# Two residual convolutions on one core: layer 2's row combinations on ScalarE and on adding transfers, reflections on GpSimd, and one buffer for statistics pieces

## The chip, the cores and the metric

The kernel runs on one core of a Trainium2 chip. A core has five engines that each work through their own list of instructions in order: TensorE (PE in the profile), VectorE (DVE), ScalarE (ACT), GpSimd (POOL) and SyncE (SP). SyncE computes nothing here: it issues the loads and stores. GpSimd issues transfers as well. The metric is the device time of one execution, in microseconds (us); lower is better.

## The reference

The input `x` is 8 images of 32 channels with 252 x 252 pixels in float32, and there is a 32 x 32 x 5 x 5 weight for each of two layers. Each layer is a group normalization, a 5x5 convolution with reflected borders and a residual addition. Cut to what is computed (the reference does the convolution through an FFT, which gives the same numbers):

```python
def gn(v):                                   # 16 groups of 2 channels, eps 1e-5, no affine part
    g = v.reshape(B, 16, 2, 252, 252)
    m, s = mean(g, over=(2, 3, 4)), var(g, over=(2, 3, 4))
    return ((g - m) / sqrt(s + 1e-5)).reshape(v.shape)

x = x + conv5x5(pad_reflect(gn(x), 2), L0_conv_weight)      # layer 1 (l = 0 in the code)
x = x + conv5x5(pad_reflect(gn(x), 2), L1_conv_weight)      # layer 2 (l = 1 in the code)
```

The mean and the variance are those of a whole image, so the convolution of an image's layer 1 can't be scaled before every pixel of the image was read once (the *statistics pass*), and layer 2 of an image can't start before layer 1 of that image is done.

## The kernel before, in words

**Layout.** An image is split by the parity of row and column into four phases. Phase and channel together make 4 x 32 = 128 partitions, and a 5x5 convolution over pixels becomes a 3x3 convolution over 126 x 126 blocks with 128 inputs and 128 outputs. The columns direction is done by three shifted matmuls (`product`, line 685). The rows direction uses a fast algorithm with six points, which makes four output block rows from six input block rows: points 1 to 4 give the sums and differences from which all four rows are made, and points 0 and 5 add what the two *outer* rows (the first and fourth of each group of four) need beside.

**Tiles and slots.** A *chunk* is 16 block rows (`ROWS`, four groups of four, `NT = 4`). An image has 8 chunks, so there are 8 images x 2 layers x 8 chunks = 128 tiles. Each has a *slot* in a list called `order`: first image 0's layer 1 alone, then chunk by chunk layer 1 of image b+1 alternating with layer 2 of image b, at last image 7's layer 2. A pair of slots in the alternating part is thus a layer 1 tile followed by a layer 2 tile or the other way about. Most tiles do points 0 and 5 with a second fast algorithm along the columns (`by_columns`): VectorE makes sums and differences of neighbouring columns (`columns`, line 619 and on), TensorE multiplies them (line 707) into the banks `sums` and `extra`, and VectorE puts the parts together (`column_parts`, lines 806 to 809).

**The input transform of a layer 2 tile** starts from `y`, the layer 1 result of 16 block rows, which stays in SBUF. It needs two sorts of row combinations:

- the *row sums* `v`, each row plus the row two further on. GpSimd's queue does these with transfers: one copies `y` to `v` (line 557), two add the shifted rows to it in place (lines 559 and 560, `accum_op=ALU.add`). `v` has one buffer, named `va`, so the copy of one layer 2 tile waits until VectorE has read the `v` of the tile before for the last time (line 609).
- the *row combinations* `u1` and `u2`: in each group of four rows, four times the second row plus the fourth, and four times the third row plus the first row of the next group. VectorE does these (`row_quads`, lines 576 and 577; `last_rows`, line 584, for the group that ends at the chunk's end).

From these VectorE makes the six points: `point2` (line 592), `point4` (596), `point3` (599), `point1` (602) and `points05` (609). For a layer 1 tile the same functions read the loaded rows `xs`, and VectorE makes `v` itself (line 567).

**The output of a tile.** ScalarE copies the finished banks of points 2 and 4 into the banks of points 1 and 3 (the *seeds*, lines 729 and 731), on top of which TensorE then adds points 1 and 3; copies points 2 and 4 out to `sd` (line 737); and VectorE makes differences and inner rows from them. In layer 1, ScalarE writes the outer rows into `y` (lines 787, 799) and squares them for layer 2's statistics (884). In layer 2, `outer_out` (line 778) has ScalarE copy the outer rows from PSUM right into the tile that is stored, four copies a tile; the inner rows go through `y` and are put into place by ScalarE in two pairs of copies, `interleave("inner", 0)` and `interleave("inner", 1)` (line 958). SyncE stores both (`send`, line 966). Every layer 1 tile also gets reflected border columns: `reflect` (lines 893 to 896), four copies by ScalarE, each of one column, 16 elements per partition; an image later its layer 2 tile reads them.

**Statistics of the next image.** While an image's layer 1 runs, the next image is read in 14 pieces of 128 x 1134 (`load_piece`, its transfer on line 254, issued by SyncE), and ScalarE passes over each twice (`piece_sums`): a sum (line 235) and a sum of squares (line 241). Chunks 0 to 6 have two pieces each, piece 2c in the layer 1 slot and piece 2c+1 in the slot after it. The pieces have two buffers (pool `spool`, tag `st`), and a piece is loaded two places ahead: right after pass p, piece p+2 is loaded.

**What sets the order.** Nothing is scheduled by a planner. `at(t, fn)` puts a function into a table under a nominal time; at the end the table is sorted by these times and each engine gets its instructions in that order (`tc.manual_schedule`). The nominal times set the order alone: what an instruction waits for while the program runs is decided by the data and by the buffers. `begin(i)` is the nominal begin of slot i; `t0` and `t1` are times within the slot. On SyncE one list holds, in order, the loads of input rows (`xs` and the last two rows `xtail`, line 143, for a chunk two layer 1 tiles on, which wait for the tile's earlier readers such as lines 577 and 584), the statistics pieces (254) and the stores (966). GpSimd's list holds the borders of loaded rows (lines 148 to 154), the addition of the residual to the weights (483), and the issue of the `v` transfers.

Of the kernel before, what the change touches and what calls it, by code (L numbers as in the profile page):

```python
# [42 lines left out]
F32 = mybir.dt.float32  # L43
BF16 = mybir.dt.bfloat16
AF = mybir.ActivationFunctionType
# [4 lines left out]
P = 128  # L50
# [6 lines left out]
def tile_conv_preact_x2(ctx: ExitStack, tc: tile.TileContext, x: bass.AP, w0: bass.AP, w1: bass.AP, out: bass.AP):  # L57
# [15 lines left out]

    const = ctx.enter_context(tc.tile_pool(name="const", bufs=1))
    xpool = ctx.enter_context(tc.tile_pool(name="xpool", bufs=2))
    spool = ctx.enter_context(tc.tile_pool(name="spool", bufs=2))
    ypool = ctx.enter_context(tc.tile_pool(name="ypool", bufs=9))
    tpool = ctx.enter_context(tc.tile_pool(name="tpool", bufs=2))
    vpool = ctx.enter_context(tc.tile_pool(name="vpool", bufs=1))
# [12 lines left out]
    def at(t: float, fn, *args, **kw):  # L92
        table.append((t, len(table), fn, args, kw))
# [151 lines left out]
    def load_piece(b: int, i: int):  # L245
        src = x[b].rearrange("ch h w -> (ch h w)").rearrange("(p n) -> p n", p=P)
        if b == 0:
            t = ypool.tile([P, PIECE], F32, tag="y", name=f"st_{b}_{i}")
        else:
            t = spool.tile([P, PIECE], F32, tag="st", name=f"st_{b}_{i}")  # L250
        parts = 3 if (b, i) == (0, NPIECE - 1) else 1
        m = PIECE // parts
        for j in range(parts):
            S.dma_start(t[:, j * m : (j + 1) * m], src[:, i * PIECE + j * m : i * PIECE + (j + 1) * m])
        pieces[b, i] = t
# [281 lines left out]
    def transform(t0: float, t1: float, b: int, l: int, c: int, free: float = -100.0, now=(0, 0, 0)):  # L537

        wi = WIN[l]
        got = {}  # L540
        sent = l == 1 and (b, c) != (0, 0)

        def source():
            if l == 0:
# [4 lines left out]
        def row_sums(add: bool):  # L549

            t, nxt = source()
            if not add:

                i = max(order.index((b, l, c)) - order.index((B - 2, 1, NCH - 2)), 0)
                got["v"] = vpool.tile([P, ROWS, wi], F32, tag=("va", "v")[i % 2], name=f"v_{b}_{l}_{c}")
                got["vt"] = got["v"].rearrange("p (t i) w -> p t i w", i=4)
                G.dma_start(got["v"], t)  # L557
            else:
                G.dma_start(got["v"][:, 0 : ROWS - 2], t[:, 2:ROWS], accum_op=ALU.add)  # L559
                G.dma_start(got["v"][:, ROWS - 2 : ROWS], nxt[:, 0:2], accum_op=ALU.add)  # L560

        def row_pairs(j0: int = 0, j1: int = NT):
            if j0 == 0:
# [67 lines left out]
        if (b, l, c) == order[0]:  # L631
            at(t0 - 33.3, row_quads, 0, 2)
            at(t0 - 31, point2, 0, 2)
            for fn in (row_pairs, point4):
                at(t0, fn, 0, 2)
            at(t0 + 0.2, row_quads, 2, 4)
            at(t0 + 0.2, row_pairs, 2, 4)
            at(t0 + 0.2, last_rows)
            at(t0 + 0.2, point2, 2, 4)
            at(t0 + 0.2, point4, 2, 4)  # L640
            at(t0 + 4.9, point1)
            at(t0 + 5.5, point3)
            at(t0 + 6.2, points05)
        else:
            if sent:
                two = begin(order.index((b, l, c)) - 2)
                at(two + 1.45, row_sums, False)
                at(two + 8.4, row_sums, True)
            else:
                at(t0, row_pairs)  # L650
            for dt, fn in ((2, row_quads), (3.2, last_rows), (3.6, point2)):
                at(t0 + dt, fn)
            at(max(t0 + 4.2, free + 9.45) if sent else t0 + 4.2, point4)
            at(max(t0 + 5.5, free + 7.8), point1)
            at(max(t0 + 5.6, free + (11.1 if by_columns(*now) else 10.25)), point3)
            at(t1, points05)
            if by_columns(b, l, c):
                at(t1 + 1.5, columns)
# [208 lines left out]
    def keep(t1: float, t2, b: int, c: int, got):  # L867
# [17 lines left out]

        def reflect():
            lo, hi = (1 if c == 0 else 0), (ROWS - 1 if c == NCH - 1 else ROWS)
            y, copy, r = got["y"], A.copy, slice(lo, hi)

            def negated(dst, src):  # L890
                A.activation(dst, src, AF.Copy, scale=-1.0)

            copy(y[:, r, 0:1], y[:, r, 1:2])
            copy(y[0:64, r, NB + 1 : NB + 2], y[0:64, r, NB : NB + 1])
            copy(y[64:128, r, NB + 1 : NB + 2], y[64:128, r, NB - 1 : NB])
            copy(y[:, r, NB + 2 : NB + 3], y[:, r, 2:3])
            if c == 0:
                negated(y[:, 0, :], y[:, 1, :])
                t = ytail[b] = small.tile([P, 2, WMAX], F32, tag="ytail", name=f"ytail_{b}")
                negated(t, y[:, 2:4, :])  # L900
            if c == NCH - 1:
                for cp in range(2):
                    negated(y[quad(cp, 0), ROWS - 1, :], y[quad(cp, 0), ROWS - 2, :])
                    negated(y[quad(cp, 1), ROWS - 1, :], y[quad(cp, 1), ROWS - 3, :])
# [33 lines left out]
    def last_but_one(b: int, c: int) -> bool:  # L938

        return (b, c) == (B - 1, NCH - 2)  # L940

    def out_tile(b: int, c: int, name: str):

        pool, tag = (spool, "st") if last_but_one(b, c) else (opool, "o")
        return pool.tile([P, NT, 2 * WOUT[1] + 2], F32, tag=tag, name=f"o_{name}_{b}_{c}")

    def store(t1: float, t0: float, b: int, c: int, got, from_y: bool):
# [23 lines left out]
        if from_y:  # L971
            for k, t in enumerate((0, 3.3)):
                at(t0 + t, interleave, "outer", k)
        for k, t in enumerate((t1 + 7.0, t1 + 7.2) if end else (t0 + 5.8, t0 + 7.8) if from_y else (t0 + 3.3, t0 + 5.8)):
            at(t, interleave, "inner", k)
        at(t0 + (4.6 if from_y else 2.6), send, "outer")
        at(t1 + 7.3 if end else t0 + 9.1, send, "inner")
# [41 lines left out]
    def begin(i: int) -> float:  # L1019

        return sum(10.2 + (own + [0.0])[j] + (late[j - 1] if j else 0.0) for j in range(i))
# [56 lines left out]
    for i, (b, l, c) in enumerate(order):  # L1078
# [36 lines left out]
        if l == 0 and b + 1 < B:  # L1115
            wide = 1 if b == 0 else 2
            if c == 0:
                for j in range(2):
                    at(begin(i - 1) + 1.0 if b > 1 else t0 + (8.0 if b else 1.0), load_piece, b + 1, j)
            if c < NPIECE // 2:  # L1120
                for j in range(2):
                    p = 2 * c + j
                    t = (t1 if wide == 2 and j else t0) + (8.6 + 2.5 * j if wide == 1 else 9.8)
                    if b == 1 and p < 4:
                        t = begin(NCH + (1, 1, 2, 2)[p]) + (9.8, 12.4, 9.8, 15.5)[p]
                    at(t, piece_sums, b + 1, p)
                    if p + 2 < NPIECE:
                        at(t + 2.6, load_piece, b + 1, p + 2)
            if c == 2:
                at(t0 + 14, fetch_weights, b + 1, 0)  # L1130
            if c == NCH - 1:
                finish_stats(b + 1, 0, *(t0 + t for t in (1.55, 4.4, 4.5, 6.9 if b else 7.7, 7.8, 8.4)))
                for j, ks in enumerate(pairs):
                    at(t0 + (9.5, 10.4, 11.3)[j], scale_points, b + 1, 0, ks)
                    at(t0 + (10.4, 12.3, 14)[j], lambda b=b, ks=ks: add_residual(G, scaled[b + 1, 0], ks))
# [43 lines left out]
```

## Time and profile before

| | us |
|---|---|
| three runs | 1912.64, 1910.19, 1912.46 |
| their median | 1912.46 |
| the profiled execution, its own time | 1912.64 |
| its span from first to last instruction | 1910.9 |
| TensorE, busy | 1850.6 (97% of the span) |
| VectorE, busy | 1736.1 (91%) |
| ScalarE, busy | 1491.1 (78%) |
| GpSimd, busy | 400.6 (21%) |

The mean clock granted to TensorE was 0.993 of full speed. Data moved at a mean of 193 GB/s: SyncE's queue took 49.6% of the time of the 16 DMA engines, GpSimd's queue 28.8%.

How to read the lines that follow: each names an engine, a line of the kernel's source, an operation, what it writes and reads (`out<-in`), and shapes as partitions x elements. In a list by time, the first column is the start and the second the duration, both in us, and a bracket at the end tells how long the engine had been idle before and for what it waited (`<-DVE sums L809`: for line 809 on VectorE). `x4` says that four instructions of that kind followed one another. SPq and POOLq are the issuing of transfers by SyncE and GpSimd.

### The profile page before, as it was taken

The page shows a single profiled execution, that of the slowest core. Times are in us where ns is not written, and L with a number is a line of the kernel's source. Part 1 is how long each engine was busy: PE and PEld are TensorE (multiplying, and loading weights), DVE is VectorE, ACT ScalarE, POOL GpSimd, SP SyncE. Part 2 cuts the span into 40 slices and gives each one's busy share as a digit, 9 for nine tenths or more (in the row PEclk, how much of TensorE's full clock was granted, in tenths as well). Part 3 has the DMA queues.
Part 4 walks back from the last instruction along what each step waited for, and adds up shares of the span by engine and source line. Part 5 has one row for each costly group of instructions (what it writes and reads, how often), then busy time and mean ns, then how long its engine had stood idle before and what let it go on. Part 6 is the DMA issues. An engine that isn't in the chain of part 4 may idle for free.

```text
span 1910.9 us, 20250 instructions
## 1 busy us (share of the span) xinstructions
PE 1850.6 (97%) x5194; PEld 961.6 (50%) x5194; DVE 1736.1 (91%) x3028; ACT 1491.1 (78%) x2661; POOL 400.6 (21%) x855
## 2 busy tenths in 40 slices
PE   5999999999999999999999999999999999999998
PEld 4444454545554555544555445554455545545455
DVE  7988799999999999989999999999999999998786
ACT  5886788878887888788897788877888866765576
POOL 4543011141112211122111311113111131110211
PEclk7999999999999999999999999999999999999999
DMA  9877588878788877987878967888878876676786
GB/s 273 205 174 183 137 212 205 193 205 217 186 207 205 195 201 180 222 211 177 214 182 202 227 178 204 190 204 204 197 207 182 210 180 142 155 180 155 179 210 136
DMA packets 207109, 369.06 MB, mean 193 GB/s; under 512 B 19088, under 2 KB 173968, under 8 KB 196752
## 3 DMA queue, kind: packets, MB, share of 16 engines
q1 hardware_dynamic: 178832, 230.73, 49.6%
q0 software_dynamic: 27600, 134.20, 28.8%
q10 hardware_dynamic: 560, 2.83, 0.4%
q8 instruction: 41, 0.67, 0.2%
q14 instruction: 76, 0.62, 0.1%
HBM read 167.15 MB, written 67.39 MB: 123 GB/s over the span
## 4 chain that ended last, share of the span: by engine, by line
PE 63%; DVE 13%; ACT 12%; issue 5%; DMA 2%; ACTq 0%; SPq 0%; DVEq 0%; POOL 0%
PE pairs L685 24%; PE m L685 19%; PE sums L685 6%; ACT o_outer L778 6%; PE sums L707 5%; PE extra L707 5%; PE extra L685 4%; DVE sd L748 1%; DMA out_dram<-o_inner 1%; ACT pairs L729 1%; ACT st L235 1%; DVE d L622 1%; DVE t L602 1%; DMA out_dram<-o_outer 1%; ACT junk L884 1%
## 5 line engine op out<-in xcount | busy, mean ns | idle before, releaser
L685 PE MATMUL pairs<-t,u 128*128 128x504 f32 (+2 forms) x1548 | 696.6, 588 | 23.6 <-ACT pairs L729 18.1
L685 PE MATMUL m<-t,u 128*128 128x508 f32 (+3 forms) x1560 | 676.2, 582 | 2.0 <-DVE u L526 2.0
L685 PEld LDWEIGHTS pairs<-t,u 128*128 128x128 f32 x1548 | 287.2, 189 | 351.8 <-issue 294.7
L685 PEld LDWEIGHTS m<-t,u 128*128 128x128 f32 x1560 | 294.7, 190 | 316.6 <-issue 294.3
L778 ACT COPY o_outer<-sums 64x512 f32<-64x512 f32 (+1 forms) x242 | 218.6, 903 | 102.9 <-PE sums L685 78.8
L707 PE MATMUL extra<-sdiff,wc 128*128 128x252 f32 (+3 forms) x680 | 173.1, 376 | 7.9 <-DVE sdiff L619 6.6
L707 PEld LDWEIGHTS extra<-sdiff,wc 128*128 128x128 f32 x680 | 125.4, 189 | 104.2 <-issue 59.7
L737 ACT COPY sd<-m 128x504 f32<-128x504 f32 (+2 forms) x258 | 136.2, 578 | 53.0 <-DVE sums L809 42.6
L748 DVE SCALAR_TENSOR_TENSOR sd<-sd,pairs 128x504 f32<-128x504 f32 (+2 forms) x258 | 163.6, 672 | 13.4 <-PE pairs L685 8.6
L958 ACT COPY o_inner<-y 64x508 f32<-64x508 f32 x248 | 165.4, 667 | 6.4 <-DMA out_dram<-o_inner 2.6
L884 ACT ACTIVATE junk<-y,negk 128x1008 bf16<-128x1008 f32 (+1 forms) x144 | 147.3, 1023 | 25.9 <-PE extra L707 15.9
L557 POOL DMA_DIRECT2D v<-y x63 | 35.7, 567 | 610.7 <-DVE t L609 555.1
L609 DVE SCALAR_TENSOR_TENSOR t<-v 128x1024 f32<-128x1024 f32 (+1 forms) x128 | 158.3, 1237 | 5.7 <-PE sums L685 5.7
L707 PE MATMUL sums<-d,u 128*128 128x252 f32 (+3 forms) x680 | 157.3, 373 | 0.0
L707 PEld LDWEIGHTS sums<-d,u 128*128 128x128 f32 x680 | 127.4, 189 | 25.1 <-issue 8.1
L685 PE MATMUL sums<-t,u 128*128 128x508 f32 (+5 forms) x312 | 133.2, 575 | 0.0
L567 DVE TENSOR_TENSOR v<-xs 128x1792 f32<-128x1792 f32 (+1 forms) x65 | 129.8, 1997 | 1.2
L148 POOL COPY xs<-xs 64x4 f32<-64x4 f32 (+3 forms) x113 | 51.3, 454 | 378.8 <-DMA xs<-in_x_dram 282.2
L241 ACT ACTIVATE st<-st,negk 128x1134 f32<-128x1134 f32 x98 | 121.7, 1242 | 3.2
L729 ACT ACTIVATE pairs<-m,means 128x504 f32<-128x504 f32 (+1 forms) x129 | 84.2, 653 | 50.4 <-PE m L685 46.5
L559 POOL DMA_DIRECT2D v<-y x63 | 54.3, 862 | 330.0 <-DMA v<-y 330.0
L159 ACT COPY xs<-xs 64x1792 f32<-64x1792 f32 (+2 forms) x97 | 109.6, 1132 | 13.5 <-POOL xs L151 11.3
(180 smaller groups left out, 2626.0 us busy)
## 6 DMA issues: line engine op xcount, KB each, us to landing
v<-y POOLq DMA_DIRECT2D x63, 1032.0 KB, 5.8
st<-in_x_dram SPq DMA_DIRECT2D x111, 567.0 KB, 6.8
v<-y POOLq DMA_DIRECT2D x63, 903.0 KB, 7.5
xs<-in_x_dram SPq DMA_DIRECT2D x96, 441.0 KB, 7.4
out_dram<-o_inner SPq DMA_DIRECT2D x241, 126.0 KB, 6.8
out_dram<-o_outer SPq DMA_DIRECT2D x226, 126.0 KB, 3.9
xs<-in_x_dram SPq DMA_DIRECT2D x44, 504.0 KB, 13.0
u<-ud SPq DMA_DIRECT2D x15, 1152.0 KB, 6.1
```

The lines of the kernel that those rows point to most:

```text
L159: copy(t[64:128, :, 0:256:2], t[0:64, :, 1:256:2])
L241: A.activation(junk, src, AF.Square, bias=negk, accum_out=acc[:, 1, i : i + 1])
L567: (V.tensor_add if l else V.tensor_sub)(v[:, r0:r1], t[:, r0 + 2 : r1 + 2], t[:, r0:r1])
L609: stt(t, got["vt"][:, :, 0:2], 4.0 if l else -4.0, got["vt"][:, :, 2:4], ALU.mult, ALU.add)
L685: T.matmul(dst, u[:, k, 2 - i, :], rhs[:, j0 + i0 : j0 + i1, i : i + wo], start=(i == 0 and not add), stop=(i == 2), skip_group_check=add,)
L707: T.matmul(dst[:, 0, use], w, rhs[:, use], start=(i == 2), stop=True, skip_group_check=(i != 2))
L729: A.activation(dst, src, AF.Identity, bias=norm[b, l][1][:, 0:1])
L737: A.copy(got["sd"][:, 1 + e], m24[e][:, 0:n])
L748: stt(d, d, -2.0, pairs13[e][:, 0:n], ALU.mult, ALU.add)
L778: (eng.copy if eng is A else eng.tensor_copy)(dst, src)
L884: A.activation(dst, src, AF.Square, bias=negk, scale=1.0 if i else -1.0, accum_out=acc[:, 1, at_ : at_ + 1])
L958: copy(got[name][halves[k], 0:n, cp : 2 * WOUT[1] : 2], got["y"][halves[cp], i : 4 * n : 4, :])
```

## The change

- `spool` has one buffer instead of two. For the pieces of images 2 to 7, piece p+1 is loaded right after pass p instead of piece p+2, and one piece instead of two is loaded ahead of the first pass (from image 3 on, 3 us later in nominal time). Image 1's pieces are still loaded two places ahead; they alternate between `spool` and the buffer `va`, which layer 2 does not need yet.
- For a layer 2 tile whose predecessor in `order` is a layer 1 tile (`sent_u`; 53 tiles: chunks 2 to 7 of image 0, all chunks of images 1 to 5, and chunks 0 to 6 of image 6) VectorE's `row_quads` and `last_rows` fall away. In their place ScalarE writes four times the second and third row of each group into a new tile `ua` (`four_times`), two slots ahead, and GpSimd issues three transfers that add the other rows to it (`outer_rows`), right behind the additions to `v`.
- The four `reflect` copies of chunks 1 to 6 are done by GpSimd instead of ScalarE.
- The pair of inner copies `interleave("inner", 1)` of a layer 2 tile whose outer rows come from PSUM takes the nominal time 3.3 us into the slot that `interleave("inner", 0)` had; `interleave("inner", 0)` moves to the time `t1 + 8.0`.
- The two output tiles of image 7's chunk 6 come from the pool of `xs` instead of `spool`.

The copies of layer 2's outer rows from PSUM (line 778) are in both kernels and are not touched. The diff, cut to its core:

```diff
-    spool = ctx.enter_context(tc.tile_pool(name="spool", bufs=2))
+    spool = ctx.enter_context(tc.tile_pool(name="spool", bufs=1))
...
-            t = spool.tile([P, PIECE], F32, tag="st", name=f"st_{b}_{i}")
+            pool, tag = (vpool, "va") if b == 1 and i % 2 else (spool, "st")
+            t = pool.tile([P, PIECE], F32, tag=tag, name=f"st_{b}_{i}")
...
         sent = l == 1 and (b, c) != (0, 0)
+        sent_u = sent and order[order.index((b, l, c)) - 1][1] == 0
...
+        def four_times():
+
+            got["u"] = vpool.tile([P, 2, NT, wi], F32, tag="ua", name=f"ua_{b}_{l}_{c}")
+            src = source()[0].rearrange("p (t i) w -> p i t w", i=4)
+            A.activation(got["u"], src[:, 1:3], AF.Copy, scale=4.0)
+
+        def outer_rows():
+            t, nxt = source()
+            u1, u2 = got["u"][:, 0], got["u"][:, 1]
+            G.dma_start(u1, t[:, 3:ROWS:4], accum_op=ALU.add)
+            G.dma_start(u2[:, 0 : NT - 1], t[:, 4:ROWS:4], accum_op=ALU.add)
+            G.dma_start(u2[:, NT - 1], nxt[:, 0], accum_op=ALU.add)
...
                 two = begin(order.index((b, l, c)) - 2)
                 at(two + 1.45, row_sums, False)
                 at(two + 8.4, row_sums, True)
+                if sent_u:
+                    at(two + 5.3, four_times)
+                    at(two + 8.5, outer_rows)
             else:
                 at(t0, row_pairs)
-            for dt, fn in ((2, row_quads), (3.2, last_rows), (3.6, point2)):
-                at(t0 + dt, fn)
+            for dt, fn in ((2, row_quads), (3.2, last_rows)):
+                if not sent_u:
+                    at(t0 + dt, fn)
+            at(t0 + 3.6, point2)
...
-            y, copy, r = got["y"], A.copy, slice(lo, hi)
+            y, copy, r = got["y"], A.copy if c in (0, NCH - 1) else G.tensor_copy, slice(lo, hi)
...
-        pool, tag = (spool, "st") if last_but_one(b, c) else (opool, "o")
+        pool, tag = (xpool, "xs") if last_but_one(b, c) else (opool, "o")
...
-        for k, t in enumerate((t1 + 7.0, t1 + 7.2) if end else (t0 + 5.8, t0 + 7.8) if from_y else (t0 + 3.3, t0 + 5.8)):
+        for k, t in enumerate((t1 + 7.0, t1 + 7.2) if end else (t0 + 5.8, t0 + 7.8) if from_y else (t1 + 8.0, t0 + 3.3)):
             at(t, interleave, "inner", k)
...
-                for j in range(2):
-                    at(begin(i - 1) + 1.0 if b > 1 else t0 + (8.0 if b else 1.0), load_piece, b + 1, j)
+                for j in range(1 if b else 2):
+                    at(begin(i - 1) + 4.0 if b > 1 else t0 + (8.0 if b else 1.0), load_piece, b + 1, j)
...
                     at(t, piece_sums, b + 1, p)
-                    if p + 2 < NPIECE:
-                        at(t + 2.6, load_piece, b + 1, p + 2)
+                    ahead = 1 if b else 2
+                    if p + ahead < NPIECE:
+                        at(t + 2.6, load_piece, b + 1, p + ahead)
```

## The prediction

> **What bounds the kernel now.** I read the page's busy table first, then what TensorE waited for between 300 and 1700 us, then one pair of slots (a layer 1 tile and a layer 2 tile) engine by engine in the timeline, then the same for the slots in which chunk 5 of layer 1 runs.
>
> ```profile
> PE 1850.6 (97%) x5194; PEld 961.6 (50%) x5194; DVE 1736.1 (91%) x3028; ACT 1491.1 (78%) x2661; POOL 400.6 (21%) x855
> ...
> PE pairs L685 <- ACT pairs L729: 11.1, 22, 0.5
> PE extra L707 <- DVE sdiff L619: 5.7, 12, 0.5
> ```
>
> TensorE is busy 97%. Its waits from 300 to 1700 us sum to 23.5 us, so no relief of VectorE can win much more there. They end on ScalarE's seed of the pairs bank (L729).
>
> ```profile
> 491.64 1.06 ACT L737 COPY sd<-m 128x504 f32<-128x504 f32 x2 [2.05 <-DVE sums L809]
> ...
> 495.05 1.15 ACT L235 ACTIVATE st<-st 128x1134 f32<-128x1134 f32 x1
> ...
> 498.68 4.43 ACT L778 COPY o_outer<-sums 64x512 f32<-64x512 f32 x4
> 503.14 0.66 ACT L729 ACTIVATE pairs<-m,means 128x508 f32<-128x508 f32 x1
> ...
> 503.85 3.67 PE L685 MATMUL pairs<-t,u 128*128 128x508 f32 x8 [0.53 <-ACT pairs L729]
> ...
> 493.94 0.70 DVE L576 SCALAR_TENSOR_TENSOR u<-y 128x516 f32<-128x516 f32 x1
> ...
> 503.14 0.69 DVE L806 TENSOR_TENSOR sums<-extra,sd 128x504 f32<-128x504 f32 x1 [0.44 <-ACT o_outer L778]
> ...
> 519.67 0.69 DVE L809 TENSOR_TENSOR sums<-sd,extra 128x504 f32<-128x504 f32 x1
> ```
>
> This pair of slots takes 28.75 us, as a loop through two engines: ScalarE from L737 (waiting for L809) to the end of L778 at 503.1, 11.5 us without a gap; then VectorE from L806 (waiting for L778) to L809 at 520.36, 17.2 us without a gap. The statistics pass L235 lies in ScalarE's half: whatever delays it delays TensorE. The row combinations that the change removes (L576 at 493.94, L577, L584) lie in VectorE's other half, which already ends in a wait for ScalarE.
>
> ```profile
> 549.50 1.14 ACT L235 ACTIVATE st<-st 128x1134 f32<-128x1134 f32 x1
> ...
> 556.66 2.50 ACT L778 COPY o_outer<-sums 64x508 f32<-64x508 f32 x4 [3.45 <-PE sums L685]
> 559.22 0.66 ACT L729 ACTIVATE pairs<-m,means 128x508 f32<-128x508 f32 x1
> ...
> 561.57 3.57 PE L685 MATMUL pairs<-t,u 128*128 128x508 f32 x8
> ...
> 537.47 3.99 SPq L143 DMA_DIRECT2D xs<-in_x_dram  x6
> 541.50 13.98 SPq L143 DMA_DIRECT2D xtail<-in_x_dram  x8
> 555.57 1.80 SPq L966 DMA_DIRECT2D out_dram<-o_inner  x4
> 557.47 0.89 SPq L254 DMA_DIRECT2D st<-in_x_dram  x2
> ...
> DMA to landing us min/median/max: 6.8/6.8/6.8
> ```
>
> Here the pass at 549.50 is piece 10 of image 3, and SyncE issues the loads of pieces 11 and 12 at 557.47, behind 14 loads of xs and xtail. The last line is the first of these two: it lands at 564.31.
>
> **One buffer for statistics pieces.** With two buffers a piece is loaded two places ahead. In the changed kernel's order of instructions on SyncE, for images 2 to 7, each place where piece p+1 was loaded now holds piece p; the passes stay where they were on ScalarE. So ScalarE waits at piece p until the landing that the trace shows for p+1. Landing less start of the pass:
> - piece 10: 14.2, 14.8, 17.3, 16.7, 15.5, 13.7 us in the six images (564.31 - 549.50 is the second), mean 15.4. Behind it ScalarE's own idle 3.45 at 556.66 and TensorE's margin of 1.69 (561.57 - 559.88) absorb 5.1. Net 10.2 x 6 = 61 us.
> - piece 12: mean 2.65, in the gapless half: x 6 = 16 us. Piece 8: 1.44, 9 us. Piece 6: 0.8, 5 us. Piece 4: between -0.8 and 0.6, but the moved copies (below) delay the pass 0.43 anyway: 2.5 us in five images.
> - piece 2: 2.9, of which 2.4 of idle time at L778 and 1.7 of margin absorb nearly all: 2.5 us. Image 2's piece 1: 5.75, and TensorE had already waited 3.0 us there: 6 us.
> - Odd pieces otherwise land 4 to 10 us ahead of their pass: nothing. Image 1 keeps two buffers (spool, and va, which layer 2 does not use yet).
>
> Sum 102 us. While SyncE waits for piece 10's passes before loading 11, the stores and xs loads behind it wait too; the xs loads wait for VectorE's L584, which is stalled as well, so I price that at nothing; without that cover it is at most the 3.9 us that those passes add.
>
> **Restarting TensorE.** At 195.57 TensorE had waited 3.0 us; its granted clock was 0.66 over 195 to 200 and the next 12 matmuls took 7.04 us for 5.34 elsewhere. So 1.7 for each of the six piece 10 stalls: 10 us, bounds 0 and 20. The Trainium skill's TensorE: Matmul & The Clock Gate, Part 1, says that one idle window of about 3.4 us drops the clock to half until a busy window has passed; by it each stall costs an estimated 1.7 us, a window at half speed, and the row agrees.
>
> **Layer 2's row combinations, 53 tiles.** Removed on VectorE: 0.70 + 0.56 + 0.29 = 1.55 us each, 82 us, in the half that waits for ScalarE: gain 0, bounds 23.5 us (all of TensorE's waits) and 0. Added on ScalarE: one 128x1032 copy with scale; nearest row L241 at 128x1134, 1.24, so 1.1 us. It stands in the layer 2 slot where one pair of inner copies (1.35) stood, which moves to the layer 1 slot, where four reflection copies (0.93) leave: +0.43 us in the gapless half, counted above for piece 4 and below the waits of the others. Idle time in the layer 2 slot (1.04 at its L729) covers the rest.
>
> **The three adding transfers** carry 1032 KB per tile in 1024 packets of 516 bytes, 64 on each of 16 engines. In the trace's packet records adding packets took 105 ns at 1032 bytes and 573 at 7224, a line that gives 66 ns at 516: 4.2 us per tile. They queue behind the v additions on POOL: the last of those lands a median 8.7 us after its issue, 15 us after the v copy was issued; ua then lands at 19 to 21. VectorE reaches point2, without its three operations, 19.7 to 21 us after that issue in chunks 2 to 4 (no wait), but at 15.5 to 16.6 in chunks 1, 5 and 7. Chunk 5 is covered by piece 10's stall. At 1 and 7 VectorE stands 2 to 4 us later than now, against 13.5 us of VectorE idle time per image: 0 to 6 us per image, I take 1: 6 us. Queued behind point2 are the differences and inner rows, for which TensorE has slots to spare.
>
> They also run where the piece loads land: DMA is busy 0.88 (512 to 527) and 0.97 (542 to 557) there, 0.59 between. At 0.88 of 15 us only 1.8 of the 4.2 us find room; 2.4 do not, and SyncE's queue shares that delay with POOL's. I take 1.5 us at each of 30 late landings (five per image): 45 us, bounds 0 and 4.2 x 30 = 126. The Trainium skill's DMA: Bandwidth & Descriptors, section Issuing engines are not separate DMA queues, says that transfers of all issuing engines run on the same 16 and interleave; the rows agree that POOL's share of time adds to SyncE's.
>
> **Reflections on GpSimd**, 192 copies of 16 elements per partition: nearest rows L153 and L154 (64x16), 0.31 and 0.51 us, 60 to 98 us on an engine idle 79%. They are read an image later: 0. They stand ahead of the next v copy, which now waits some 13 us for L609 anyway. Beside VectorE: L567 has median 2.02 us and maximum 2.21 though it shares its time with such copies, which themselves range from 0.18 to 1.91: the copies lose, not VectorE. The Trainium skill's SBUF — State Buffer, section Who interferes with whom, says that a VectorE instruction with two SBUF inputs and a GpSimd one that reads SBUF block each other for the whole instruction, whoever comes second; by it VectorE could lose an estimated 0.3 us per copy, 58 us, which the row does not show.
>
> **Tail and first piece.** The output tiles of image 7's chunk 6 take xs buffers that are free by then: 0. Piece 0 moves 3 us later and had 21 us to spare: 0.
>
> **Sum.** The profiled execution's own time is 1912.64 (span 1910.9 and 1.7 around it), 0.2 above the median of the runs. 102 + 10 + 45 + 6 = 163, less some overlap of stalls (TensorE cannot pay twice for one stretch; 5): 2070 us.
>
> **Rivals.**
> - The adding transfers find room: 1912.6 + 102 + 10 = 2025. For it: 0.59 between the busy stretches; against it: ua starts some 15 us after the v copy, in the busy one.
> - The SyncE queue takes their full price: 1912.6 + 102 + 10 + 126 = 2151. For it: SyncE's queue is never empty from 537 to 564; against it: half of the packets should go the other way.
> - Only piece 10 counts, the rest going into ScalarE's idle 2.05 at L737: 1912.6 + 61 + 10 = 1984. Against it: that idle stands before the pass, not after.
> - VectorE's 1.55 us wins: down to 1912.6 - 23.5 = 1889. It decides if the loads land within the 0.43 us by which the pass moves, above all at piece 10 (15.4 now); for that its load would have to overtake the xtail loads, and the order on SyncE speaks against it.
>
> **How the numbers follow.** Forecast 0.44, room 0.24, full price 0.15, piece 10 alone 0.09, VectorE's gain 0.06, and 0.02 for gains and waits in balance; some 0.2% (4 us) is what a measurement of this kernel can tell from no change. Range 1972 to 2150: it takes in piece 10 alone without the clock's 10 (1974) and leaves out the last two and the upper half of the full price. Faster 0.06, same 0.02, slower 0.92.
>
> **What would show it.** Right: waits of ScalarE's L235 pass for the DMA of st, longest about 12 to 18 us, once per image from image 2; TensorE waiting some 10 us behind ScalarE's seeds there; granted clock under 1 in those slices; DMA share up; VectorE's busy time 80 us less. Wrong: if ScalarE hardly waits for st, or if VectorE's waits for ua are the longest.

## The result, and the profile after

| | before | after |
|---|---|---|
| median of the runs, us | 1912.46 | 2104.77 (2100.25 to 2106.85, 4 runs) |
| ratio, with its 95% interval | 1 | 1.1005 [1.0986, 1.1025] |
| span of the profiled execution | 1910.9 | 2103.1 |
| mean granted clock of TensorE | 0.993 | 0.967 |

The changed kernel is 10% slower, 192 us. The prediction's 2070 lies 35 us below, its range (1972 to 2150) holds the result. The total is near; its parts, as the experiments show, are not all what the prediction said.

The busy table of the page, and after it the waits of TensorE from 300 to 1700 us:

```profile
PE 1901.7 (90%) x5194; PEld 974.3 (46%) x5194; DVE 1659.1 (79%) x2869; ACT 1496.8 (71%) x2522; POOL 646.0 (31%) x1206
...
PE pairs L705 <- ACT pairs L749: 104.1, 34, 10.8
```

VectorE has 77 us less to do, as foreseen, and the kernel is slower all the same: TensorE falls from 97% to 90%. Where it waited 11.1 us for ScalarE's seed (L749 is the L729 of before), it now waits 104.1, up to 10.8 at a time.

Two sorts of waits are new. The first lines are from ScalarE's waits over the whole span (us in all, how often, the longest), the others from VectorE's:

```profile
ACT st L235 <- DMA st<-in_x_dram: 145.1, 29, 16.1
...
DVE sums L826 <- ACT o_outer L798: 168.2, 40, 11.2
DVE t L607 <- DMA ua<-y: 113.3, 28, 10.7
DVE t L607 <- DMA ua<-ytail: 45.5, 6, 8.5
```

The statistics pass L235 waits 145 us for its pieces, against 2.9 in the kernel before, and VectorE's `point2` (L607) waits 159 us for `ua`. The profile alone can't say which of the two sets the time, because they fall into the same stretches. VectorE's largest wait, 168 us for L798, follows ScalarE's stalls; it is 137 us in a run without `ua` (the first below).

Piece 10 of image 3, the slot that the prediction showed of before, in the timelines of SyncE, ScalarE and TensorE:

```profile
580.89 7.39 SPq L143 DMA_DIRECT2D xs<-in_x_dram  x6
588.33 11.09 SPq L143 DMA_DIRECT2D xtail<-in_x_dram  x8
599.46 1.87 SPq L986 DMA_DIRECT2D out_dram<-o_inner  x4
601.43 8.31 SPq L255 DMA_DIRECT2D st<-in_x_dram  x2
...
606.75 1.15 ACT L235 ACTIVATE st<-st 128x1134 f32<-128x1134 f32 x1 [12.00 <-DMA st<-in_x_dram]
...
613.56 5.53 PE L705 MATMUL pairs<-t,u 128*128 128x508 f32 x8 [6.70 <-ACT pairs L749]
```

The load of piece 10 is issued at 601.43, after fourteen loads of input rows that take SyncE from 580.89 to 599.42 and a store; it lands at 606.73; ScalarE has stood still for 12.00 us, and TensorE for 6.70. Of the 18.5 us of the fourteen loads, issuing itself takes 10.4; in most of the rest SyncE waits until earlier loads of rows have landed (its waits from 578 to 602 us):

```profile
SPq L143 <- DMA xs<-in_x_dram: 7.6, 3, 2.9
```

The eight matmuls that follow take 5.53 us, against 3.67 for the eight of the same kind in the kernel before. The granted clock in these stretches (after each stretch and its length, the busy time of PE, PEld, DVE, ACT and POOL; the last three columns are clock, data engines' share and GB/s):

```profile
606.00:609.00 3.00, 0.86 (x3) 0.04 (x1) 0.00 (x0) 2.22 (x3) 0.00 (x0) 1.00 0.39 163
609.00:612.00 3.00, 0.00 (x0) 0.00 (x0) 0.00 (x0) 2.96 (x7) 1.73 (x2) 0.75 0.53 121
612.00:616.00 4.00, 2.44 (x3) 1.17 (x4) 3.11 (x6) 3.93 (x8) 0.00 (x0) 0.50 1.06 233
616.00:620.00 4.00, 4.00 (x11) 2.16 (x10) 4.00 (x6) 1.97 (x4) 2.30 (x3) 0.83 1.00 227
620.00:624.00 4.00, 4.00 (x16) 2.78 (x15) 3.90 (x9) 3.97 (x6) 1.20 (x2) 1.00 1.16 149
```

### The profile page after: what moved, and what is told of

Same layout as the page of the kernel before. It is cut to its first block, busy times and chain, and to the rows that moved or that the text cites. A ratio compares the mean times of both kernels' runs of the same rounds, so it can differ in the third digit from the quotient of the medians.

```text
span 2103.1 us, 20506 instructions
## 1 busy us (share of the span) xinstructions
PE 1901.7 (90%) x5194; PEld 974.3 (46%) x5194; DVE 1659.1 (79%) x2869; ACT 1496.8 (71%) x2522; POOL 646.0 (31%) x1206
## 4 chain that ended last, share of the span: by engine, by line
DMA 27%; PE 21%; DVE 15%; issue 14%; ACT 10%; SPq 5%; POOL 4%; ACTq 0%; DVEq 0%; POOLq 0%
PE pairs L705 9%; DMA st<-in_x_dram 7%; PE m L705 6%; DMA v<-y 5%; DMA xs<-in_x_dram 5%; DMA ua<-y 5%; ACT o_outer L798 4%; DMA ua<-ytail 4%; SPq L143 3%; PE extra L705 2%; DMA out_dram<-o_inner 2%; SPq L986 2%; PE sums L705 2%; ACT junk L904 2%; ACT st L235 1%
## 5 line engine op out<-in xcount | busy, mean ns | idle before, releaser
L705 PE MATMUL pairs<-t,u 128*128 128x504 f32 (+2 forms) x1548 | 736.6, 616 | 134.8 <-ACT pairs L749 129.5
L705 PEld LDWEIGHTS pairs<-t,u 128*128 128x128 f32 x1548 | 301.1, 199 | 490.8 <-issue 307.6
L798 ACT COPY o_outer<-sums 64x512 f32<-64x512 f32 (+1 forms) x242 | 215.2, 889 | 59.8 <-DMA out_dram<-o_inner 23.5
L235 ACT ACTIVATE st<-st 128x1134 f32<-128x1134 f32 x98 | 112.5, 1148 | 145.6 <-DMA st<-in_x_dram 145.1
L826 DVE TENSOR_TENSOR sums<-extra,sd 128x512 f32<-128x512 f32 (+1 forms) x85 | 58.9, 693 | 169.4 <-ACT o_outer L798 168.2
L607 DVE TENSOR_TENSOR t<-ua 128x516 f32<-128x516 f32 x53 | 36.8, 694 | 160.7 <-DMA ua<-y 113.3
L624 DVE SCALAR_TENSOR_TENSOR t<-v 128x1024 f32<-128x1024 f32 (+1 forms) x128 | 158.4, 1238 | 4.2 <-PE sums L705 4.2
L749 ACT ACTIVATE pairs<-m,means 128x504 f32<-128x504 f32 (+1 forms) x129 | 84.3, 653 | 69.8 <-PE m L705 53.1
## 6 DMA issues: line engine op xcount, KB each, us to landing
xs<-in_x_dram SPq DMA_DIRECT2D x44, 504.0 KB, 12.3
```

Source lines behind the costliest of these rows:

```text
L235: A.activation(junk, src, AF.Identity, accum_out=acc[:, 0, i : i + 1])
L624: stt(t, got["vt"][:, :, 0:2], 4.0 if l else -4.0, got["vt"][:, :, 2:4], ALU.mult, ALU.add)
L705: T.matmul(dst, u[:, k, 2 - i, :], rhs[:, j0 + i0 : j0 + i1, i : i + wo], start=(i == 0 and not add), stop=(i == 2), skip_group_check=add,)
L749: A.activation(dst, src, AF.Identity, bias=norm[b, l][1][:, 0:1])
L798: (eng.copy if eng is A else eng.tensor_copy)(dst, src)
L826: V.tensor_add(half(sums05, 0, both, ne), m12, even)
```

## The experiments

The change has four parts that can be done or undone alone: **A**, one buffer for the pieces and their later loads; **I**, the moved inner copies; **R**, the reflections on GpSimd; **U**, `ua` in place of VectorE's row combinations. U needs the room that A frees: two piece buffers and `ua` together take 3.9 KB per partition more than there is. So U was not tried on the kernel before itself. The kernel before measured 1911.6 to 1912.3 beside these runs.

**A alone** (`one_buffer`): the kernel before with the diff's lines on `spool`, `load_piece` and the two output tiles.

```diff
-    spool = ctx.enter_context(tc.tile_pool(name="spool", bufs=2))
+    spool = ctx.enter_context(tc.tile_pool(name="spool", bufs=1))
...
-                    if p + 2 < NPIECE:
-                        at(t + 2.6, load_piece, b + 1, p + 2)
+                    ahead = 1 if b else 2
+                    if p + ahead < NPIECE:
+                        at(t + 2.6, load_piece, b + 1, p + ahead)
```

> The kernel before with only the statistics pieces changed: one buffer, pieces loaded one place ahead, image 1's odd pieces in va, the last two output tiles from the pool of xs. VectorE keeps the row combinations, ScalarE the reflections. Theory of the prediction (the single buffer is the largest term: 102 us of waits and 10 us of clock): about 2022 us, 2010 to 2035, with waits of L235 of 12 to 17 us at piece 10 once per image. Rival (VectorE's waits for ua, 159 us in the changed kernel's trace, are the larger term and most piece waits lie in their shadow): below 1985 us. Piece 4 tells more: in the changed kernel it waits 4 to 5 us per image; if SyncE's place in the order alone is the cause, it waits as long here; if the traffic of ua is, it waits under 1 us.

Measured: 2004.06 us, ratio 1.0478 [1.0461, 1.0496], 92 us. From the timelines of SyncE and ScalarE of this run:

```profile
562.24 7.20 SPq L143 DMA_DIRECT2D xs<-in_x_dram  x6
569.49 11.52 SPq L143 DMA_DIRECT2D xtail<-in_x_dram  x8
581.11 1.83 SPq L967 DMA_DIRECT2D out_dram<-o_inner  x4
583.03 9.12 SPq L255 DMA_DIRECT2D st<-in_x_dram  x2
...
589.16 1.15 ACT L235 ACTIVATE st<-st 128x1134 f32<-128x1134 f32 x1 [14.80 <-DMA st<-in_x_dram]
```

The wait at piece 10 is there without `ua`: 16.5, 14.8, 16.4, 14.7, 17.0 and 12.9 us in the six images. From one seed L729 to the seed two slots later, the pairs with piece 10 are 14.3, 11.3, 13.2, 12.3, 14.1 and 10.2 us longer than before, 75 us in all. Image 2's piece 1 makes 6.7. At piece 4 of images 3 to 7 L235 waits 0 to 0.8 us, against 3.9 to 4.9 in the changed kernel, so that wait comes from the rest of the change. The time lies 18 us under the theory's 2022, a little outside its range, and above the rival's 1985. What U does alone is not told by it.

**The change without U** (`no_ua`): `sent_u = False`.

> The changed kernel with VectorE's row combinations put back (no ua, no four_times, no outer_rows); the single buffer, GpSimd's reflections and the moved inner copies stay. Against the run with the single buffer alone it shows what reflections and moved copies cost: the prediction says nothing but a few us at piece 4 (within 5 us). Against the changed kernel (2104.8) it shows what ua costs: the prediction has 51 us for it (2045 to 2060 for this run if the changed kernel's 2104.8 is taken as given, 2022 by the prediction's own sum); the rival says that ua costs at least 100 us (below 2005).

Measured: 2025.7, ratio 1.059 [1.0571, 1.0609]. That is the 2022 of the prediction's own sum, but by other terms: I and R add 21.6 us to A, more than the 5 allowed, and U adds 79 on top, more than its 51 and less than the rival's 100.

**U's traffic without its wait** (`ua_unread`): the changed kernel in which `ua` is made and read by nobody.

```diff
-            got["u"] = vpool.tile([P, 2, NT, wi], F32, tag="ua", name=f"ua_{b}_{l}_{c}")
+            got["ua"] = vpool.tile([P, 2, NT, wi], F32, tag="ua", name=f"ua_{b}_{l}_{c}")
...
-                if not sent_u:
-                    at(t0 + dt, fn)
+                at(t0 + dt, fn)
```

> The changed kernel with ua written by ScalarE and by the three adding transfers as before, but nobody reads it: VectorE makes the row combinations itself again into the tile u12. All of ua's traffic is there, no wait for it. If ua's cost is the traffic that delays the other loads (the prediction's 45 us of 51), the time stays near the changed kernel, 2085 to 2105 us; if it is VectorE's wait for ua to land, it falls to the time of the run without ua, within 10 us of it.

Measured: 2078.16, ratio 1.0864 [1.0846, 1.0883]. Neither end: of U's 79 us, 52 come without anyone reading `ua` (traffic and ScalarE's copy) and 27 from the wait. L235 waits 162 us here, against 112 without U, so the price is paid at the pieces, above all at pieces 2, 4, 6 and 10: at piece 4 of images 3 to 7 it waits a mean 2.8 us here and 0.0 without U.

**ScalarE loads its own pieces** (`act_loads`), from behind its own pass, past SyncE's list:

```diff
-            S.dma_start(t[:, j * m : (j + 1) * m], src[:, i * PIECE + j * m : i * PIECE + (j + 1) * m])
+            eng.dma_start(t[:, j * m : (j + 1) * m], src[:, i * PIECE + j * m : i * PIECE + (j + 1) * m])
...
-                        at(t + 2.6, load_piece, b + 1, p + ahead)
+                        at(t + 2.6, load_piece, b + 1, p + ahead, A if b else S)
```

> The changed kernel, still with one buffer, but pieces 1 to 13 of images 2 to 7 are loaded by a transfer that ScalarE issues itself, 2.6 us of nominal time after its pass over the piece before, so that they stand behind no load of input rows on SyncE's list. Theory of the prediction: the waits of L235 vanish (a load takes 3.5 to 7 us, the next pass comes 10 us later or more), and with them 102 to 112 us and perhaps part of the 45: 1950 to 2000 us. Rival (ua bounds): 2050 us or more, with VectorE's waits for ua standing as before or longer.

Measured: 2079.49, ratio 1.0879 [1.0848, 1.0911]. The prediction's theory falls here: the waits for pieces do go, and only 25 us come back. The first line is from the costliest groups of this run's page, the others are waits of VectorE and ScalarE:

```profile
L235 ACT ACTIVATE st<-st 128x1134 f32<-128x1134 f32 x98 | 112.3, 1146 | 20.4 <-DMA st<-in_x_dram 19.4
...
DVE t L607 <- DMA ua<-y: 212.4, 42, 12.9
DVE t L607 <- DMA ua<-ytail: 47.2, 6, 9.2
...
ACT o_outer L798 <- DMA out_dram<-o_inner: 82.2, 25, 12.0
```

125 us of waits for pieces have turned into 100 more of VectorE for `ua` and into 82 of ScalarE (23.5 in the changed kernel), which waits at the copies of the outer rows for the store of inner rows. The second wait was in nobody's theory.

**I alone** (`inner_only`): the kernel before with one line of the diff.

```diff
-        for k, t in enumerate((t1 + 7.0, t1 + 7.2) if end else (t0 + 5.8, t0 + 7.8) if from_y else (t0 + 3.3, t0 + 5.8)):
+        for k, t in enumerate((t1 + 7.0, t1 + 7.2) if end else (t0 + 5.8, t0 + 7.8) if from_y else (t1 + 8.0, t0 + 3.3)):
```

> The kernel before with only the two pairs of inner copies moved as in the change. Theory A (formed from the trace of the run with ScalarE's own loads, where ScalarE waits 82 us at the copies of the outer rows for stores of inner rows): the first inner copy now stands ahead of the outer copies, so the inner tile takes the output buffer that comes free first and the outer tile, in the half of the loop without idle time, has to wait for the store of inner rows, which stands behind the loads of xs on SyncE's list. Then this alone costs 10 to 22 us: 1922 to 1934, with waits of the outer copies for the DMA of o_inner, and the last image's slots longer. Theory B (the moved copies cost only their 0.43 us of ScalarE's time, as the prediction says, and the 21.6 us between the runs without ua and with the single buffer alone come from GpSimd's reflections): 1912 to 1917.

Measured: 1976.23, ratio 1.0342 [1.0325, 1.036]: 64 us, three times what theory A had, and far from theory B. Once per image, in the slot of piece 10:

```profile
547.55 7.00 SPq L143 DMA_DIRECT2D xs<-in_x_dram  x6
554.59 12.02 SPq L143 DMA_DIRECT2D xtail<-in_x_dram  x8
566.66 1.86 SPq L966 DMA_DIRECT2D out_dram<-o_inner  x4
...
570.91 2.46 ACT L778 COPY o_outer<-sums 64x508 f32<-64x508 f32 x4 [6.69 <-DMA out_dram<-o_inner]
```

The first inner copy now comes before the outer copies of its tile. There are two output buffers. In the list of instructions before, the outer tile of a chunk waits for the store of the last chunk's outer tile, the inner one for that of the inner tile; after, each waits for the other's. The inner store comes later, and here it stands behind the fourteen loads. These waits are 56 us in 9 places. They don't explain all: by the seeds, images 3 to 7 take 9.3 us longer each, of which the slot of piece 10 makes 3.4 (with the one behind it). The rest is 0.6 to 1.4 us in each of six other pairs of slots, where the two copies moved in take 1.35 us of ScalarE in the half of the loop without idle time; the last 24 slots add 10.5.

**The change without I** (`inner_back`): the same line turned back.

> The changed kernel with the inner copies back at their old places; single buffer, ua and GpSimd's reflections stay. Theory A: 10 to 25 us less than the changed kernel, 2080 to 2095, since at piece 10 the wait for the piece covers the wait for the store. Theory B: 2100 to 2108.

Measured: 2094.14, ratio 1.0947 [1.0928, 1.0967]. The 64 us of I shrink to 11 inside the change, as theory A has it. In the changed kernel ScalarE does not wait for an inner store until the last image: at piece 10 the wait for the piece, behind the same fourteen loads, covers it. With the pieces on ScalarE's own list (`act_loads`) it is there, 10.7 to 12.0 us in five of the six images.

**R alone** (`reflect_only`): the kernel before with GpSimd's `tensor_copy` for the reflections of chunks 1 to 6.

> The kernel before with only the reflections of chunks 1 to 6 on GpSimd. The prediction says nothing: 1907 to 1918. Rival 1: four copies (0.93 us) leave the half of ScalarE's loop that has no idle time, 30 of the 48 such tiles stand in it, so up to 28 us are won: 1885 to 1905. Rival 2: the copies stand on GpSimd's list ahead of the v copy and wait there for ScalarE to write y (GpSimd waited 40 to 57 us for that in two of the runs), so v comes later: 1920 to 1935.

Measured: 1909.5, ratio 0.9992 [0.9983, 1.0002]: no change, as predicted; both rivals fall. ScalarE's 31.6 us less of work (1491.1 to 1459.5 busy) turn mostly into waiting at the very next step. ScalarE's waits, before and with R:

```profile
ACT extra L711 <- PE extra L707: 17.7, 33, 1.1
```

```profile
ACT extra L711 <- PE extra L707: 43.0, 48, 1.1
```

The reflections stood just ahead of L711, which waits for TensorE. And VectorE's busy time is 1734.1 us with R, 1736.1 without.

**Pieces by ScalarE, inner copies back** (`act_inner`), and the same **with ua first** (`act_inner_first`): the second moves `ua`'s making ahead of the `v` copy.

```diff
-                    at(two + 5.3, four_times)
-                    at(two + 8.5, outer_rows)
+                    at(two + 0.2, four_times)
+                    at(two + 1.4, outer_rows)
```

> The changed kernel with pieces loaded by ScalarE's own transfers and the inner copies back at their old places. Theory A: the waits of the outer copies for stores of inner rows (82 us in the run with ScalarE's loads alone) go, and the saving of the piece loads that this run hid comes out: 1990 to 2040. Theory B, or VectorE's wait for ua as what bounds (260 us of waits in that run): within 15 us of 2079.

> As the run before, and ua is made first: four_times moves to 0.2 us and outer_rows to 1.4 us into the slot two ahead, so that ua's three adding transfers are issued ahead of the v copy instead of behind the v additions. If what VectorE waits for is ua's place at the end of GpSimd's queue, its waits for ua (over 200 us) go and the time falls by 30 us or more against the run before it, to 1940 to 2000. If the data engines have no room for the traffic at all, the wait moves from ua to v, and the time is within 15 us of the run before it.

Measured: 2059.93, ratio 1.0779 [1.0752, 1.0807], and 2049.05, ratio 1.0723 [1.0704, 1.0742]. The first lies between its two expectations, 19.5 us under 2079 and far above 2040. With ScalarE's waits down to 30 us for pieces and 12 for stores the kernel is still 148 us slower than before, and VectorE waits 281 us for `ua`. With `ua` first that wait is gone, and VectorE waits 242 us for `v` instead (this line, and 51.4 for `v<-ytail`):

```profile
DVE t L611 <- DMA v<-y: 190.9, 46, 10.6
```

That is 11 us of gain. The place of `ua` in GpSimd's queue is not the cause.

**The same without U** (`act_no_ua`) **and with ua unread** (`act_unread`):

> The run with ScalarE's own piece loads and the inner copies at their old places (2059.9), without ua: VectorE makes the row combinations as before. What is left of the change is one buffer, and GpSimd's reflections. If the place behind SyncE's loads is all that one buffer costs: 1912 to 1935, and then ua alone costs 125 us or more once piece waits no longer cover it, against the 51 of the prediction. If a single buffer costs in itself (loads issued later, ScalarE's issuing): 1950 or more.

> As the run before, but ua is written by ScalarE and the adding transfers and read by nobody. The time between the run without ua and this one is what ua's traffic and ScalarE's copies cost; from this one to the 2059.9 of the run that reads ua is what waiting for it costs. The prediction, with 45 of its 51 us for traffic, says that this run is nearer to the one that reads ua; the rival (VectorE's waits for ua, 281 us in that run's trace, are the cost) that it lies within 30 us of the run without ua.

Measured: 1942.15, ratio 1.0166 [1.0149, 1.0183], and 1977.87, ratio 1.0349 [1.0334, 1.0364]. The first lies between its two expectations: 62 of A's 92 us go when the pieces don't stand on SyncE's list, and 30 stay. (R is in this kernel too; it was worth nothing alone, and in this setting it was not measured.) Some of what remains is the same place again: once per image ScalarE waits for a store.

```profile
572.32 1.33 ACT L978 COPY o_inner<-y 64x508 f32<-64x508 f32 x2 [4.81 <-DMA out_dram<-o_inner]
```

In this setting U costs 118 us: 36 without a reader, 82 for the wait. The rival is nearer: uncovered, the wait is the larger part of what U costs, and this run lies 36 us from the one without `ua` (a little over the rival's 30) and 82 from the one that reads it. The 36 are not waits for pieces, which are 23.5 us here and 23.8 without `ua`. ScalarE's waits for stores of inner rows make 10 more (37.6 against 27.5); the rest was not located.

What sets the wait is shown by one tile of `act_inner` (GpSimd's and VectorE's timelines):

```profile
564.84 0.57 POOL L559 DMA_DIRECT2D v<-y  x1 [11.60 <-DVE t L624]
570.95 2.01 POOL L573 DMA_DIRECT2D ua<-y  x1
...
590.48 0.70 DVE L607 TENSOR_TENSOR t<-ua 128x516 f32<-128x516 f32 x1 [10.70 <-DMA ua<-y]
596.54 1.22 DVE L624 SCALAR_TENSOR_TENSOR t<-v 128x1032 f32<-128x1032 f32 x1
...
598.07 0.57 POOL L559 DMA_DIRECT2D v<-y  x1 [2.38 <-DVE t L624]
```

The `v` copy starts when VectorE's `points05` (L624) has read the old `v`; `ua` comes behind `v`; `point2` waits for `ua`; `points05` ends 7.3 us after `point2` begins; then the next `v` copy starts. That is a closed loop. Its medians in this run: 23.3 from the copy to `point2`, 7.3 to the end of `points05`, 0.3 to the next copy, some 31 us, against 28.75 for a pair of slots. Without `ua` (`act_no_ua`) the first term is 20.8. Over the 53 tiles the mean time between `v` copies is 31.6 us, against 30.0 with `ua` unread: 53 times the difference is 83 us, so the 82 of the wait lie in these rounds. That one delay feeds the next is read from the trace; no run breaks the loop, as a second buffer for `v` would.

**Half of ua** (`act_half`): as `act_inner`, but ScalarE and one transfer make `u1` alone; VectorE makes `u2`.

> As the run with ScalarE's own piece loads, the inner copies at their old places and ua read (2059.9), but only u1 is made by ScalarE and one adding transfer; VectorE makes u2 itself. Loop theory, from that run's trace: the next v copy waits for VectorE's points 0 and 5, these come 7.3 us after point2, point2 waits for ua, and ua lands a median 23.2 us after the v copy was issued (8.3 after the v additions): 23.2 + 7.3 and some 0.5 of issuing make 31, more than the 29.3 between v copies without ua. With half the transfers ua should land about 19.2 us after the copy, ahead of VectorE, which comes to point2 at 20.9 without ua: the 82 us of waiting go nearly altogether and half of the 36 us of traffic stays, 1955 to 1970 us. Rival (each byte of ua costs alike, no threshold): half of the 118 us that ua costs here, 2001, between 1990 and 2010.

Measured: 1980.03, ratio 1.0362 [1.0344, 1.0379], 38 us over the run without `ua`; midway between the two expectations, 10 us from the range of each. `ua` lands a median 20.1 us after the copy (expected 19.2), `point2` begins at 21.2, and the median time between `v` copies is 29.2, as without `ua`. In single tiles the wait stays: VectorE's list has 97 us for `ua` in 25 places, the longest 10.0. The unchanged time between copies speaks for a threshold, and the single tiles say that it is not sharp; the time of the kernel alone does not decide between the two. What scatters `ua`'s landing from tile to tile was not told apart.

No version beat the kernel before.

## Why the prediction was right, and where it was wrong

**The ledger.** One after the other: A 92, I and R 22, U's traffic 52, U's wait 27, in all 193. Each by itself: A 92, I 64, R -2, U 118 (with ScalarE loading the pieces), in all 272. The prediction's terms: 112 for A with its clock, nothing for I and R beyond that, 45 for traffic, 6 for the wait, less 5. That its sum, 158, came within 35 of the measured 192, and inside the range, is partly luck: taken one after the other, A was put 20 too high, and U 28, I and R 22 and the overlap 5 too low. And had the parts not hidden each other, the time would have left the range: at the fourteen loads of chunk 5 a piece and an output buffer wait at the same time, and only the longer wait counts (64 us of I shrink to 11). `ua`, by the tile's loop, waits in the same stretches (U's 118 are 79 in the change).

**One buffer: right in place and size.** Piece 10 waits 12.9 to 17.0 us alone (forecast 13.7 to 17.3) and costs 75 us with its clock, forecast 61 and 10. Image 2's piece 1 cost 6.7 (forecast 6). Piece 12 was wrong: 16 us forecast, no wait in any image; it landed 1.9 to 3.3 us before its pass in all six images. The forecast took landings from the trace of before, and behind the stall at piece 10 everything stands otherwise against SyncE's list; why by just so much stays open. Piece 11 was misread: the forecast has odd pieces land 4 to 10 us early, but by its own rule (the landing of piece 12 in the trace of before) piece 11 came between 0.9 us before its pass and 1.4 us after it. It did no harm, since no image waits at piece 11 with A alone.

**The clock.** 1.86 us more for the eight matmuls at 613.56 (forecast 1.7 per stall). TensorE's busy time in all grew 51 us, against 10 forecast: the trace has the clock at 0.50 in 25 stretches of 3 to 17 us, against 4 in the kernel before, and not in six alone. Half of TensorE's busy time in these stretches is an estimated 45 us, against 6 before, so some 39 of the 51 are the clock's. The Trainium skill's TensorE: Matmul & The Clock Gate, Part 1, says that the clock halves after an idle window of some 3.4 us and comes back after a busy one; the rows above agree, with 0.50 from 612 to 616 and 1.00 again from 620.

**"+0.43 us in the gapless half": the step that failed for the inner copies.** The prediction counted the copies' time and not the order in which the two output buffers are taken. Alone that is 64 us. It stood in no rival. In the changed kernel it comes out only where no piece is waited for, in the last 24 slots, which were forecast to cost nothing and take 19 us longer (14 without `ua`; 7 with the inner copies back).

**"I take 1: 6 us" for VectorE's wait: the term that was mis-sized.** The prediction let `ua` land 19 to 21 us after the `v` copy; it landed at a median of 23.1 in the changed kernel, 7.3 us behind the median landing of `v`, 15.8, where 4.2 were forecast. The price per packet was right (516 bytes took a median 66 ns, as the line gave; GpSimd's share went from 550 to 799 us of the 16 engines, 4.7 per tile), though the three transfers carry 258, 193.5 and 64.5 KB, 516 KB per tile and not the 1032 that the prediction names; its price went by the packets and is not touched. That the packets share the engines with SyncE's while they run is the likely reason for the late landing; no run separates it. And the prediction set the delay against VectorE's idle time per image, although the `v` copy waits for VectorE's last read: by the loop above, a delay comes back every tile and is not absorbed once. Its own mark for being wrong, that VectorE's waits for `ua` be the longest, was met in the sum, 159 us against 145 for the pieces, though the longest single wait, 16.1, is a piece's.

**The traffic's 45** measured 52 in the change and 36 with the pieces on ScalarE's list. Size right. The mechanism, late landings, fits the first: with `ua` unread L235 waits 50 us longer for pieces than without U. It does not fit the second, where these waits do not grow. Both figures hold ScalarE's copy as well (53 of 1.07 us), which no run has without the transfers.

**Reflections: right.** The Trainium skill's SBUF — State Buffer, Who interferes with whom, has VectorE's instructions with two SBUF inputs and GpSimd's reads block each other, for which the prediction gave an estimate of 58 us. The run has 0.9992 and the same busy time on VectorE: the measurement decides for the row.

**VectorE's relief** was put at nothing, and nothing speaks against it: with 77 us less of work VectorE waits longer. But no run has the relief without `ua`, so this is not shown by itself. R alone shows the like of ScalarE, whose saved time became a wait for TensorE. One reading was too broad: of TensorE's 23.5 us of waits before, 11.1 end on ScalarE's seed, not all.

## What to carry to other kernels

When a change has several parts, price each part alone and then ask which of them wait at the same place: their prices are not added, and taking one away may give little back (25 of 125 us here). A buffer that is freed by the consumer of the transfer behind it makes a closed loop: add a transfer to it and compare the loop's round with the slot, not the landing with one reader. Moving an instruction also moves its claim on a buffer: look at which store each tile waits for after the move.

## What was not expected of the hardware

One list held up loads that had nothing to do with each other. In the trace of the changed kernel every transfer on SyncE's list names one of eight semaphores, in turn, that tells of its landing, and none is issued before the transfer that had the semaphore last has landed. At piece 10 of image 3 the load of rows at 583.91 lands at 596.14, and the load eight places on is issued at 596.15, with 3 us of standing still before it. So of the 18.5 us of the fourteen loads (7.39 and 11.09) 8.1 are no issuing, and the load of the piece stands behind them, though it lands 5.3 us after its own issue. The fourteen issues take 0.31 to 1.69 us each; why some take so long was not found. The Trainium skill's DMA: Bandwidth & Descriptors, Issuing engines are not separate DMA queues, says that issuing from several engines saves only the sequencer's time, usually small against the transfer. Here more was saved: the same loads issued by ScalarE, at 0.33 to 0.38 us each, did not stand behind the fourteen, and 62 of A's 92 us went.
